# Graph convolution with residual and layer norm: comparison columns in a PSUM bank, and picks in six turns of two and two sets

## The chip, the core and the metric

The kernel runs on one core of a Trainium2 chip. The core has a matrix engine (TensorE, PE in the profile; its weight loads are PEld), VectorE (DVE), ScalarE (ACT), GpSimd (POOL) and SyncE (SP), which run side by side and wait for one another through semaphores. Matmul results land in PSUM, which this kernel divides into eight banks of 512 fp32 columns on 128 partitions; everything else lies in SBUF. The metric is the device time of one execution in microseconds. A run's program is fixed before it starts: each engine works through its own list of instructions in that list's order.

## The reference

There are 12,500 nodes with 128 features and 400,000 edges sorted by destination. Each edge takes its source's row, multiplies it by one of two weight matrices by its type, and is summed into its destination; then come the self term, a relu, the residual and a layer norm.

```
Xs = X[src]
m_data = Xs @ W_data.T + b_data
m_ctrl = Xs @ W_control.T + b_control
msg = jnp.where((edge_types == 0)[:, None], m_data, m_ctrl)
agg = jax.ops.segment_sum(msg, dst, num_segments=X.shape[0])
out = relu(agg + (X @ W_self.T + b_self))
x = layernorm(x + out)
```

## The kernel before

Sums over edges are linear, so the kernel first adds up source rows by destination and type, and multiplies by the weights afterwards. Rows of x are kept in SBUF as three bf16 parts whose sum is the fp32 value (`x3`: block of 128 nodes, part, feature).

The 3,125 chunks of 128 edges fall into 25 groups of 125. A part of each group's chunks has its source rows fetched by GpSimd's indirect DMAs (`msg`, line 887; 945 of them). The others, twenty chunks at a time, form 109 **pairs** (windows of 2,560 edges), whose source rows come out of SBUF by matmul. For a pair VectorE works out where each edge goes: it compares every edge's block number with a column of block numbers (`O`, 2,000 wide, `block_matrix`), gets ranks from a prefix sum that TensorE makes of `O` (`before`, line 634, in the bank `side`; VectorE reads it in `ahead`, line 642, and goes on with `product`, the folds of lines 656 and 661, `found`, `rank`, `rm`), and multiplies (`rv`, line 713). TensorE then **puts** the edges into slots (line 726), ScalarE copies the slots (`cell`), a DMA writes them out and another spreads them over the partitions, and VectorE turns them into one-hot columns (`pick`, line 790). This is prepared one to three pairs ahead.

With the pick columns TensorE **picks** (line 990): 25 sets of slots, each set four matmuls that write 32 partitions each and 384 columns (three parts of a row), of which the last set has two matmuls. ScalarE copies the picked rows from PSUM to bf16 (`emsg`, lines 1004 and 1006). VectorE makes a selection per set by comparing the codes of its slots with `code_col` (`esel`, 172 wide for one set, line 541 of the helper `select`), and TensorE **adds** (line 803): three matmuls a set, rows times selection, into a bank `sums`. At the end of a pair VectorE adds the bank to the accumulators (`acc`, line 876, 172 columns). Fetched chunks go the same way, with `psel` (compared with `near_col`) and matmuls 48 wide.

A pair's picks run in five turns of 5, 5, 5, 4 and 5 sets (`bounds`); the half set goes with the fourth turn. A turn picks two sets into a tile of two banks (`got2`), two or three into a tile of three banks (`got3`), and ScalarE makes one copy of each. In the same turn the sets of the turn before are added; a pair's last sets are added in the first turn of the next pair. Each of the two tiles has one buffer, so a turn's picks wait for the copy of the turn before. The eight banks are: `side` 1, `sums` 2, `got2` 2, `got3` 3. Selections are made in three instructions, for 10, 9 and 6 sets.

What sets the order: the code gives each piece of work a place within its pair (`merged`, fractions of a pair; for example the second selection 0.305, `ahead` 0.31, the third selection 0.36), some VectorE work is chained in a fixed order (`in_turn`), and a scheduler then decides each engine's list before the run, by priority and by its own estimate of when things are ready. Work may therefore stand far ahead of the place at which the code writes it.

## Time and profile before

| | us |
|---|---|
| median of 3 runs (1672.21 to 1674.59) | 1673.62 |
| the profiled execution | 1674.38 |
| its span (first to last instruction) | 1672.7 |
| of it 0 to 100: rows are split into parts, first pairs prepared | VectorE busy 84.8, TensorE 45.7 |
| of it 1600 to 1672.7: last pairs, last rows written | VectorE busy 43.1, TensorE 62.4 |
| mean granted TensorE clock | 0.994 |

Outside its span the profiled execution has 1.7 us. In the long middle one pair follows another every 14 us or so, and every engine's load is nearly even over it. In the rows below, the number behind an x is a count; behind a bar stand the busy time in us and the mean duration of one instruction in ns, and behind the next bar how long the engine stood idle before such instructions, and what ended the idling.

### The profile page before, as it was taken

How to read it: one execution, taken by the hardware profiler on the slowest of the kernel's cores; microseconds unless marked ns; L12 is line 12 of the kernel's file. 1: busy time of each engine (PE TensorE's matmuls, PEld its weight loads, DVE VectorE, ACT ScalarE, POOL GpSimd, SP SyncE). 2: the span in 40 equal slices, each digit the busy share in tenths (PEclk: the TensorE clock that was granted, in tenths of full speed). 3: DMA queues.
4: the chain of work that ended last, by engine and by line, in shares of the span. 5: the costliest groups of instructions: out<-in, count | busy, mean ns of one | idle time of the engine just before them, and what ended most of it. 6: DMA issues, size and time to landing. Idle time of an engine off the chain costs nothing.

```text
span 1672.7 us, 67703 instructions
## 1 busy us (share of the span) xinstructions
PE 1551.5 (93%) x27966; PEld 1222.6 (73%) x27966; DVE 1569.9 (94%) x4078; ACT 1224.0 (73%) x2056; POOL 1239.8 (74%) x1022
## 2 busy tenths in 40 slices
PE   1699999999999999999999999999999999999998
PEld 0377777777777777777777777777777777777776
DVE  9799999999999999999999999999999999999983
ACT  7687777777777777677777778767786777668674
POOL 1277777887887887778777887878887787877881
PEclk9899999999999999999999999999999999999999
DMA  7944444554455454544554454554545454544441
GB/s 218 278 148 139 130 150 132 153 154 135 142 160 151 137 158 132 155 135 133 159 149 140 137 155 138 151 160 132 159 125 163 137 160 129 160 138 136 137 134 42
DMA packets 147605, 246.05 MB, mean 147 GB/s; under 512 B 35565, under 2 KB 114264, under 8 KB 147288
## 3 DMA queue, kind: packets, MB, share of 16 engines
q1 hardware_dynamic: 99128, 142.50, 25.6%
q0 software_dynamic: 48160, 99.14, 22.4%
q8 instruction: 221, 3.62, 0.9%
q14 instruction: 96, 0.79, 0.1%
HBM read 224.04 MB, written 17.52 MB: 144 GB/s over the span
## 4 chain that ended last, share of the span: by engine, by line
DVE 42%; PE 41%; issue 6%; ACT 5%; DMA 3%; DVEq 1%; POOL 0%; SPq 0%; ACTq 0%; POOLq 0%
PE sums L803 18%; PE got L990 13%; DVE esel L541 6%; DVE prod L656 4%; PE side L1111 4%; DVE prod L648 4%; DVE pick L790 3%; DVE O L541 3%; ACT emsg L1004 2%; DVE rv L713 2%; DVE prod L627 2%; DVE psel L541 2%; DVE rm L541 2%; DVE found L666 2%; PE side L726 2%
## 5 line engine op out<-in xcount | busy, mean ns | idle before, releaser
L887 POOL DMA_INDIRECT msg<-rows,idx_g x945 | 1169.2, 1237 | 311.5 <-issue 122.8
L1004 ACT CAST emsg<-got 128x768 bf16<-128x768 f32 x1090 | 965.3, 930 | 295.4 <-PE got L990 286.4
L803 PE MATMUL sums<-esel,emsg 128*128 128x172 bf16 x7848 | 687.2, 238 | 5.4 <-DVE acc L876 4.3
L803 PEld LDWEIGHTS <-emsg 128*128 128x128 bf16 x7848 | 569.0, 97 | 118.0 <-issue 109.5
L990 PE MATMUL got<-x,pick 128*32 128x384 bf16 x10682 | 582.1, 330 | 11.6 <-ACT emsg L1004 6.2
L990 PEld LDWEIGHTS <-pick 128*32 128x32 bf16 x10682 | 246.4, 96 | 140.1 <-issue 20.1
L541 DVE TENSOR_TENSOR esel<-code_col,code 128x1720 bf16<-128x1720 bf16 x327 | 292.9, 896 | 5.6 <-PE sums L803 5.3
L803 PE MATMUL sums<-psel,msg 128*128 128x48 bf16 x2835 | 161.8, 184 | 11.1 <-DVE acc L876 11.0
L803 PEld LDWEIGHTS <-msg 128*128 128x128 bf16 x2835 | 133.8, 97 | 20.0 <-issue 17.0
L656 DVE TENSOR_TENSOR prod<-prod 128x1200 bf16<-128x1200 bf16 x218 | 136.2, 625 | 9.7 <-issue 4.5
L648 DVE TENSOR_TENSOR prod<-O,ahead 128x2000 bf16<-128x2000 bf16 x109 | 130.7, 1199 | 2.8
L541 DVE TENSOR_TENSOR O<-cell_col,blk 128x2000 bf16<-128x2000 bf16 x109 | 129.8, 1190 | 0.5 <-ACT blk L443 0.5
L790 DVE TENSOR_SCALAR pick<-pick,lane_f 128x3200 bf16<-128x3200 bf16 x109 | 112.7, 1034 | 2.6 <-DMA pick<-there 2.6
L726 PE MATMUL side<-rv,O 128*128 128x64 bf16 x2180 | 85.4, 196 | 31.4 <-DVE rv L713 30.9
L963 POOL DMA_INDIRECT both<-rows,idx x55 | 65.5, 1190 | 65.7 <-DVE mv L1125 27.5
L726 PEld LDWEIGHTS <-O 128*128 128x128 bf16 x2180 | 80.1, 100 | 38.9 <-DVE rv L713 27.7
L541 DVE TENSOR_TENSOR psel<-near_col,near 128x1200 bf16<-128x1200 bf16 x125 | 95.9, 767 | 0.0
L627 DVE TENSOR_TENSOR prod<-prod 128x500 bf16<-128x500 bf16 x327 | 94.3, 288 | 0.8
L713 DVE TENSOR_TENSOR rv<-rm,vals 128x1280 bf16<-128x1280 bf16 x109 | 89.3, 820 | 0.0
L622 DVE TENSOR_TENSOR prod<-O 128x1000 bf16<-128x1000 bf16 x109 | 73.9, 678 | 2.4 <-DVE bits L701 1.0
L876 DVE TENSOR_TENSOR acc<-acc,sums 128x172 f32 (+2 forms) x234 | 65.4, 280 | 2.7 <-PE sums L803 2.5
L642 DVE TENSOR_REDUCE ahead<-side 128x100 bf16<-128x200 f32 x109 | 39.1, 359 | 26.0 <-PE side L634 24.8
(197 smaller groups left out, 1528.1 us busy)
## 6 DMA issues: line engine op xcount, KB each, us to landing
pick<-there SPq DMA_DIRECT2D x108, 800.0 KB
msg<-rows,idx_g POOLq DMA_INDIRECT x945
acc<-acc_start SPq DMA_DIRECT2D x23, 640.0 KB
rows<-x SPq DMA_DIRECT2D x6, 1344.0 KB
xs<-in_x_dram SPq DMA_DIRECT2D x99, 62.5 KB
out_dram<-h SPq DMA_DIRECT2D x99, 62.5 KB
xt<-in_x_dram SPq DMA_DIRECT2D x6, 896.0 KB
cnt<-cnt_start SPq DMA_DIRECT2D x22, 160.0 KB
```

The source lines that it names most:

```text
L541: ins = nc.vector.tensor_tensor(sel.rearrange("p n (w t) -> p n w t", t=2), col[:rows].rearrange("p (o w t) -> p o w t", o=1, t=2).to_broa ...
L622: return nc.vector.tensor_add(h[:, :2 * CQ], s["O"][:, :2 * CQ], s["O"][:, 2 * CQ:])
L627: return nc.vector.tensor_add(h[:, to:to + n], h[:, a:a + n], h[:, b:b + n])
L648: return nc.vector.tensor_tensor(s["prod"][:, :, :NCELL], s["O"], s["ahead_b"].rearrange("p (o j) -> p o j", o=1).to_broadcast([P, EC, NCE ...
L656: return nc.vector.tensor_add(prod[:, :, :h], prod[:, :, :h], prod[:, :, h:2 * h])
L713: placed[:] = [nc.vector.tensor_tensor(rv.rearrange("p c v (r t) -> p c v r t", t=2), s["rm"].rearrange("p c (o r t) -> p c o r t", o=1, t ...
L726: nc.tensor.matmul(s["rk"][:m, :2 * CAP], s["held"][:, c * NCELL:c * NCELL + m], s["rv"][:, c].rearrange("p v r -> p (v r)"), start=(c == ...
L790: return nc.vector.tensor_scalar(t, t, lane_f, None, op0=OP.is_equal)
L803: last = nc.tensor.matmul(out, msg[:, j * D:(j + 1) * D], sel, start=(start and j == 0), stop=stop, skip_group_check=True)
L887: return nc.gpsimd.indirect_dma_start(out=msg, out_offset=None, in_=rows3[:, :], in_offset=bass.IndirectOffsetOnAxis(ap=codes["p", g][0][: ...
L990: last = nc.tensor.matmul(ps[CAP * a:CAP * (a + 1), :], slots[w]["pick"][:, a * NQ + q, :], x3[:, 4 * q + a - a0].rearrange("p j d -> p (j ...
L1004: s["out"] = nc.scalar.copy(msg[:, :n], ps[:, :n, :3 * D])
```

## The change

It does three things.

1. A new pool holds one PSUM bank, `cols`. The five tables that VectorE compares with (two of `cell_cols`, `rank_col`, `code_col`, `near_col`) are copied there once, as fp32 words, and `select` reads them from there as bf16. The compared codes still come from SBUF.
2. The picks run in six turns of four sets, each turn with two tiles of two banks (`got0`, `got1`). The half set is picked in the fifth turn as six matmuls of 128 columns, into the 128 columns that are left free in three of the four banks; ScalarE copies it with two instructions in place of one. The selections are made for 8, 8 and 9 sets. What was tied to the fourth and fifth turn (put, spread, codes) is tied to the fifth and sixth.
3. Each pick is ordered behind the pick before it and given high priority (`behind`), over a whole tile.

The banks are now `side` 1, `sums` 2, `got0` 2, `got1` 2, `cols` 1.

```diff
@@ -218,6 +218,7 @@
     ps1 = ctx.enter_context(tc.tile_pool(name="ps1", bufs=1, space=PSUM))
     ps2 = ctx.enter_context(tc.tile_pool(name="ps2", bufs=2, space=PSUM))
     psg = ctx.enter_context(tc.tile_pool(name="psg", bufs=1, space=PSUM))
+    psc = ctx.enter_context(tc.tile_pool(name="psc", bufs=1, space=PSUM))
 
     def side():
 
@@ -351,6 +352,18 @@
     rank_col = table(CAP, 0, "rank_col")
     code_col = table(2 * EW, 1, "code_col")
     near_col = table(2 * PW, 0, "near_col")
+    cols = psc.tile([P, 512], FP, name="cols")
+
+    def on_psum(t):
+        n = t.shape[1] // 2
+        at = cols[:, used[0]:used[0] + n]
+        used[0] += n
+        nc.vector.tensor_copy(at, t.bitcast(FP))
+        return at.bitcast(BF)
+
+    used = [0]
+    cell_cols = [on_psum(t) for t in cell_cols]
+    rank_col, code_col, near_col = on_psum(rank_col), on_psum(code_col), on_psum(near_col)
     ident_b = keep.tile([P, P], BF, name="ident_b")
     nc.vector.tensor_copy(ident_b, ident)
     lane_f = keep.tile([P, 1], FP, name="lane_f")
@@ -765,9 +778,9 @@
             keep_codes()
             s["own"][3]()
 
-        s["tiled"] = {4: [put, spread], 5: [turn_codes, keep_codes]}
+        s["tiled"] = {5: [put, spread], 6: [turn_codes, keep_codes]}
         if w % 2:
-            s["tiled"][5] = [lambda: (turn_codes(), own_before())]
+            s["tiled"][6] = [lambda: (turn_codes(), own_before())]
             s["own_turn"] = own_turn
         wide = NCELL + EC
         s["begin"] = {"blocks": block_matrix, "same": same_lane, "tens": tens, **{
@@ -971,12 +984,12 @@
 
         g, i = each_e[w]
         s = {"sel": {}, "msg": {}}
-        bounds = [0, 5, 10, 15, 19, NQ - 1]
+        bounds = [0, 4, 8, 12, 16, 20, NQ - 1]
         turns = len(bounds) - 1
 
         def choose(q0, n, prev=None):
 
-            sel = sp.tile([P, 10, 2 * EW], BF, name="esel", bufs=3)[:, :n]
+            sel = sp.tile([P, 9, 2 * EW], BF, name="esel", bufs=3)[:, :n]
             sel, ins = select(sel, code_col, slots[w]["code"][:, q0:q0 + n], prev)
             for k in range(n):
                 s["sel"][q0 + k] = sel[:, k]
@@ -985,25 +998,38 @@
         lead = 0 if w % 2 else 2
         half_rows = slice(CAP * lead, CAP * lead + OVF)
 
-        def pick(ps, q, a0=0, a1=4):
+        def behind(first, f):
+
+            if first is None:
+                return f()
+            with after(first), tc.high_priority():
+                return f()
+
+        def pick(ps, q, a0=0, a1=4, last=None):
             for a in range(a0, a1):
-                last = nc.tensor.matmul(
+                last = behind(last, lambda: nc.tensor.matmul(
                     ps[CAP * a:CAP * (a + 1), :], slots[w]["pick"][:, a * NQ + q, :],
                     x3[:, 4 * q + a - a0].rearrange("p j d -> p (j d)"), start=True, stop=True, skip_group_check=True,
-                )
+                ))
             return last
 
-        def rows(q, n, room, half=False):
-            ps = psg.tile([P, room, 512], FP, name=f"got{room}")
-            msg = two.tile([P, room, 3 * D], BF, name=f"emsg{room}")
-            for k in range(n):
-                last = pick(ps[:, k, :3 * D], q + k)
-                s["msg"][q + k] = msg[:, k, :]
+        def rows(q, k, half=False):
+            ps = psg.tile([P, 2, 512], FP, name=f"got{k}")
+            msg = two.tile([P, 2, 3 * D], BF, name=f"emsg{k}")
+            last, ends = None, (2 - k) if half else 0
+            for j in range(ends):
+                for a in range(lead, lead + 2):
+                    last = behind(last, lambda: nc.tensor.matmul(
+                        ps[CAP * a:CAP * (a + 1), j, 3 * D:], slots[w]["pick"][:, a * NQ + NQ - 1, :],
+                        x3[:, 4 * (NQ - 1) + a - lead, 2 * k + j, :], start=True, stop=True, skip_group_check=True,
+                    ))
+            for j in range(2):
+                last = pick(ps[:, j, :3 * D], q + j, last=last)
+                s["msg"][q + j] = msg[:, j, :]
+            s["out"] = nc.scalar.copy(msg, ps[:, :, :3 * D])
             if half:
-                last = pick(ps[:, n, :3 * D], NQ - 1, lead, lead + 2)
-            s["out"] = nc.scalar.copy(msg[:, :n], ps[:, :n, :3 * D])
-            if half:
-                nc.scalar.copy(s["msg"][NQ - 1][half_rows, :], ps[half_rows, n, :3 * D])
+                to = s["msg"][NQ - 1][half_rows, 2 * k * D:(2 * k + ends) * D]
+                nc.scalar.copy(to.rearrange("p (k d) -> p k d", d=D), ps[half_rows, :ends, 3 * D:])
             return last
 
         def add(q0, q1):
@@ -1015,17 +1041,17 @@
 
         def unit(t):
 
-            if t == 3:
+            if t == 4:
                 assert not spare
                 if "both" in slots[w]:
                     slots[w]["last"] = two.tile([P, 3 * D], BF, name="last", bufs=1)
                 s["msg"][NQ - 1] = slots[w]["last"]
-            paced(w + (t + 0.5) / turns, rows(bounds[t], 2, 2))
+            paced(w + (t + 0.5) / turns, rows(bounds[t], 0, t == 4))
             if t == 1 and w > 0 and w % 2 == 0:
                 spare.append(lambda: spare_rows(w))
-            gate = rows(bounds[t] + 2, bounds[t + 1] - bounds[t] - 2, 3, t == 3)
+            gate = rows(bounds[t] + 2, 1, t == 4)
             if t == 0:
-                choose(0, 10)
+                choose(0, 8)
                 gates = ending() or [gate]
             while counts:
                 c = counts.pop(0)
@@ -1037,8 +1063,6 @@
             if t > 0:
                 gates = add(bounds[t - 1], bounds[t])
             paced(w + (t + 1) / turns, gates[0])
-            if t == 2:
-                paced(w + (t + 1) / turns, gates[-1])
             for u in tiled.get(t, []):
                 u()
             if t == 0 and w + 1 < pairs and "own_turn" in slots[w + 1] and w > 0:
@@ -1057,7 +1081,7 @@
             accumulate(place_of(g, 2 * i + 1), acc_rows(g, 0, 2), s["ps"], EW, EW)
             return gates
 
-        chosen_later = [lambda prev=None, q=q, n=n: choose(q, n, prev) for q, n in ((10, 9), (19, NQ - 19))]
+        chosen_later = [lambda prev=None, q=q, n=n: choose(q, n, prev) for q, n in ((8, 8), (16, NQ - 16))]
         return evenly([lambda t=t: unit(t) for t in range(turns)]), end, chosen_later
 
 
@@ -1154,7 +1178,7 @@
             at["rk"] = side()
             s[2]()
 
-        return {5: [lambda: None, turn, s[3]]}, [(0.1, before), (0.33, s[1])]
+        return {6: [lambda: None, turn, s[3]]}, [(0.1, before), (0.33, s[1])]
 
     def check_all():
```

What this does to the lists of instructions, at three places in the middle of the program:

VectorE, around the read of the prefix sum (`ahead`), before. TENSOR_LOAD and ISA read a window's place into a register; `prod` 20x60, 20x30 and 20x14 are the folds.

```order
L642 TENSOR_REDUCE ahead<-side 128x100
L648 TENSOR_TENSOR prod<-O,ahead 128x20x100
L859 TENSOR_LOAD place_i
L859 ISA x2
L656 TENSOR_TENSOR prod<-prod 128x20x60
L541 TENSOR_TENSOR esel<-code_col,code 128x1032
L656 TENSOR_TENSOR prod<-prod 128x20x30
L541 TENSOR_TENSOR esel<-code_col,code 128x1720
L661 TENSOR_TENSOR prod<-prod 128x20x14
L666 TENSOR_REDUCE found<-prod 128x20
L612 TENSOR_TENSOR prod<-blk_21792,blk_184 128x20x20
L671 CAST rank<-found 128x40
```

The same place now.

```order
L554 TENSOR_TENSOR esel<-cols,code 128x1376
L655 TENSOR_REDUCE ahead<-side 128x100
L661 TENSOR_TENSOR prod<-O,ahead 128x20x100
L872 TENSOR_LOAD place_i
L872 ISA x2
L669 TENSOR_TENSOR prod<-prod 128x20x60
L554 TENSOR_TENSOR esel<-cols,code 128x1548
L669 TENSOR_TENSOR prod<-prod 128x20x30
L674 TENSOR_TENSOR prod<-prod 128x20x14
L679 TENSOR_REDUCE found<-prod 128x20
L625 TENSOR_TENSOR prod<-blk_22380,blk_193 128x20x20
L684 CAST rank<-found 128x40
```

Before, the third selection of a pair (1032) and the first of the next (1720) stand between the folds; now only the third (1548) does, and the last two folds follow each other directly.

VectorE, at the end of a pair: the accumulations (`acc`, `cnt`), before. `prod` 2x100 and 100 are the last two folds of the next prefix sum's input.

```order
L627 TENSOR_TENSOR prod<-prod 128x2x100
L541 TENSOR_TENSOR esel<-code_col,code 128x1548
L627 TENSOR_TENSOR prod<-prod 128x100
L876 ISA
L876 TENSOR_TENSOR acc<-acc,sums 128x2x86
L876 ISA
L876 TENSOR_TENSOR cnt<-cnt,sums 64x120
L876 ISA
L876 TENSOR_TENSOR acc<-acc,sums 128x2x40
L541 TENSOR_TENSOR psel<-near_col,near_21340 128x1200
```

The same place now; the row `esel` 1376 that leads the listing above follows directly behind it.

```order
L554 TENSOR_TENSOR esel<-cols,code 128x1376
L640 TENSOR_TENSOR prod<-prod 128x2x100
L581 TENSOR_SCALAR om_all_202<-slot_col,side 128x70
L640 TENSOR_TENSOR prod<-prod 128x100
L581 TENSOR_SCALAR om_all_202<-slot_col,side 128x70
L889 ISA
L889 TENSOR_TENSOR acc<-acc,sums 128x2x86
L554 TENSOR_TENSOR psel<-cols,near_20270 128x1200
L889 ISA
L889 TENSOR_TENSOR cnt<-cnt,sums 64x120
L889 ISA
L889 TENSOR_TENSOR acc<-acc,sums 128x2x40
```

Ahead of `ahead` there was one selection (1548, the pair's second); now there are two, the pair's first and second (1376 each). The first has moved here from behind the previous pair's third.

TensorE, where it makes the prefix sum (`ltri` is its weight), before.

```order
L990 LDWEIGHTS pick
L990 MATMUL got_19830<-x_104,pick 32x384
L634 LDWEIGHTS ltri
L634 MATMUL side<-prod,ltri 128x2x25
L634 LDWEIGHTS ltri
```

And now, at such a place.

```order
L816 LDWEIGHTS emsg_20272
L816 MATMUL sums<-esel,emsg_20272 128x172
L647 LDWEIGHTS ltri
L647 MATMUL side<-prod,ltri 128x2x25
L647 LDWEIGHTS ltri
```

Before, it stands right behind a turn's picks in 67 of the 109 pairs, and behind adds in 8; now behind picks in 38, and behind adds in 51.

## The prediction

> **What bounds the kernel now.** I read the page's busy shares first, then the busy time of the long middle, then who waits for whom there, because shares over the whole span mix the start and the tail with it.
>
> ```profile
> PE 1551.5 (93%) x27966; PEld 1222.6 (73%) x27966; DVE 1569.9 (94%) x4078; ACT 1224.0 (73%) x2056; POOL 1239.8 (74%) x1022
> DVE 42%; PE 41%; issue 6%; ACT 5%; DMA 3%; DVEq 1%; POOL 0%; SPq 0%; ACTq 0%; POOLq 0%
> 100.00:1600.00 1500.00, 1443.41 (x26322) 1141.15 (x26312) 1442.01 (x3691) 1111.18 (x1894) 1180.70 (x955) 1.00 0.48 144
> DVE ahead L642 <- PE side L634: 22.3, 33, 1.9
> DVE esel L541 <- PE sums L803: 0.9, 2, 0.8
> PE side L574 <- DVE om_all L568: 15.4, 18, 1.0
> PE sums L803 <- DVE acc L876: 15.0, 29, 1.9
> PE got L990 <- ACT emsg L1004: 4.3, 7, 1.3
> ```
>
> The second row is the chain that ended last, by engine; the third is the stretch from 100 to 1600 us (busy PE, PEld, DVE, ACT, POOL); the others are waits in that stretch (us, times, longest). TensorE and VectorE are both busy for 96% of it, and the chain passes between them. VectorE is the tighter one, since TensorE's busy time covers waits inside its pipelined matmuls. VectorE stands idle for 1500 − 1442.0 = 58.0 us, and the largest item is `ahead` waiting for TensorE's prefix sum, 22.3 us. ScalarE and GpSimd have 389 and 319 us to spare. So the time is VectorE's work plus what VectorE waits for, and a change must shorten one of the two.
>
> **Part 1: the columns in PSUM.** 670 instructions change their first source: `O`, `rm` and three `esel` 109 times each, `psel` 125 times.
>
> ```profile
> L541 DVE TENSOR_TENSOR O<-cell_col,blk 128x2000 bf16<-128x2000 bf16 x109 | 129.8, 1190 | 0.5 <-ACT blk L443 0.5
> L541 DVE TENSOR_TENSOR esel<-code_col,code 128x1720 bf16<-128x1720 bf16 x109 | 114.0, 1046 | 5.5 <-PE sums L803 5.3
> L541 DVE TENSOR_TENSOR esel<-code_col,code 128x1548 bf16<-128x1548 bf16 x109 | 103.9, 953 | 0.1
> L541 DVE TENSOR_TENSOR esel<-code_col,code 128x1032 bf16<-128x1032 bf16 x109 | 75.0, 688 | 0.0
> L876 DVE TENSOR_TENSOR acc<-acc,sums 128x172 f32 x109 | 35.3, 324 | 2.7 <-PE sums L803 2.5
> L876 DVE TENSOR_TENSOR acc<-acc,sums 128x240 f32 x16 | 6.2, 390 | 0.0
> L839 DVE TENSOR_TENSOR acc<-acc 128x280 f32<-128x280 f32 x24 | 10.5, 436 | 0.0
> ```
>
> From 1032 to 2000 columns a selection grows by 502 ns, 0.519 ns a column, with a fixed 152 ns. No row reads bf16 from PSUM. The nearest are `acc`, one fp32 source in PSUM (`sums`) and one in SBUF: 0.97 ns a column and, at 1.04, 145 ns fixed for 172 columns; L839, both sources in SBUF, has 436 − 280 × 1.04 = 145 as well. So the place of a source moves the fixed part by nothing that shows, and I take 0. The bounds: the fixed part could fall to 145, 670 × 7 ns = 5 us less; or the rate could fall to the fp32 rows' one column per 1.04 ns, twice as slow.
>
> [...]
>
> [...]
>
> The five copies that fill `cols` cost some 0.1 us each, once, 0.5 us. Whatever GpSimd gains from a freer VectorE cannot count: it is idle for a fifth of the middle, and no fetched chunk is among the waits above.
>
> **Part 2: VectorE's list.** The selections still cover 25 × 172 columns in three instructions, so their work is unchanged. Two things in their place are not.
>
> ```profile
> 815.67 0.77 DVE L541 TENSOR_TENSOR psel<-near_col,near 128x1200 bf16<-128x1200 bf16 x1
> 816.36 0.35 DVE L642 TENSOR_REDUCE ahead<-side 128x100 bf16<-128x200 f32 x1
> 816.75 1.20 DVE L648 TENSOR_TENSOR prod<-O,ahead 128x2000 bf16<-128x2000 bf16 x1
> 817.99 0.79 DVE L656 TENSOR_TENSOR prod<-prod 128x1200 bf16<-128x1200 bf16 x1
> ```
>
> An instruction normally starts 0.08 us before the end of the one in front (815.67 + 0.77 against 816.36); one that needs its neighbour's result starts 0.04 us after it (816.75 + 1.20 against 817.99). A dependent neighbour therefore costs 0.12 us. Over the whole list such neighbours go from 489 to 556, mostly because the first selection no longer stands between the last fold and `found`: 67 × 0.12 = **+8.0 us** of VectorE time, on the tighter engine, with nothing to hide it.
>
> Against this, the moved selection changes when VectorE asks for the prefix sum. Between `ahead` and `rv` stood 1720 and 1032, now 1548; ahead of `ahead` stood 1548, now 1376 twice. With 0.08 us of overlap each, 0.966 + 0.608 − 0.873 = 0.70 us per pair moves from behind `ahead` to in front of it. VectorE reaches `ahead` 0.70 us later in its own list, without more work in all.
>
> **Part 3: TensorE's list.**
>
> ```profile
> 803.30 0.39 PE L803 MATMUL sums<-psel,msg 128*128 128x48 bf16 x9
> 803.61 1.00 PE L990 MATMUL got<-x,pick 128*32 128x384 bf16 x20
> 804.54 1.29 PE L803 MATMUL sums<-esel,emsg 128*128 128x172 bf16 x15
> 805.67 0.24 PE L803 MATMUL sums<-psel,msg 128*128 128x48 bf16 x3
> 805.83 1.00 PE L990 MATMUL got<-x,pick 128*32 128x384 bf16 x18
> ...
> 63.97 0.51 PE L990 MATMUL got<-x,pick 128*32 128x384 bf16 x8
> 64.41 0.54 PE L803 MATMUL sums<-esel,emsg 128*128 128x172 bf16 x5
> ```
>
> Starts count here, since the ends are modelled. Five sets take 804.54 − 803.61 = 0.93 us until the next kind of work, two sets 0.44: 0.163 a set and 0.11 for the change of work behind them. Nine `psel` matmuls take 0.31 until picks follow, three take 0.16: 0.025 each, and 0.085 for the change into picks. A batch of picks thus costs 0.20 us beyond its sets. In the two lists batches go from 630 to 727: +97 × 0.20 = 19.4 us. But 78 batches used to break inside a set of four, which then streams twice, and now none does: −78 × 0.163 = −12.7 us. The half set's six narrow matmuls stream the columns of the two wide ones; 0. Together +6.7 us on TensorE, half a percent of its work, and it lies beside VectorE's work, under 56.6 us of TensorE idling (1500 − 1443.4). If that cover were gone it would cost 6.7 us.
>
> For the prefix sum TensorE is earlier: in the two turns in front of it there are eight picks (0.33 us) and three adds fewer (three of 15 in 1.13 us, 0.22); six adds (0.45 us) now precede it in 51 of 109 pairs, 0.21 on average. Net 0.34 us earlier. With VectorE's 0.70 us, the margin at `ahead` grows by some 1.0 us against waits of 22.3 / 33 = 0.68 us on average and 1.9 at most. Nearly all the short ones go, the long ones keep up to 0.9; some of the waits will turn up later, at `acc` or at a gap that VectorE reaches sooner. I take **−15 us** of the 22.3, bounds 0 and −22.3.
>
> **Part 4: ScalarE.**
>
> ```profile
> L1004 ACT CAST emsg<-got 128x768 bf16<-128x768 f32 x654 | 512.3, 801 | 270.5 <-PE got L990 262.5 <-PE sums L803 1.3 <-ACT emsg L1004 1.0
> L1004 ACT CAST emsg<-got 128x1152 bf16<-128x1152 f32 x436 | 489.5, 1123 | 24.9 <-PE got L990 23.9 <-PE side L747 0.2 <-issue 0.2
> L1006 ACT CAST both<-got 64x384 bf16<-64x384 f32 x55 | 26.5, 481 | 0.0
> ```
>
> Per pair six copies of 801 and four of 1123 (9298 ns) become twelve of 801 (9612). The half set's copy of about 480 becomes two, 256 and 128 columns wide; at (1123 − 801) / 384 = 0.84 ns a column and 157 fixed they take 372 + 264. That is +0.47 us a pair, 52 us in all, inside the 389 us that ScalarE idles. What it can cost is the second rival's case.
>
> **Sum.** 1674.38 (profiled, 0.76 above the median) − 15 + 8.0 + 0.5 + 0 = 1667.9, I say **1668 us**, 0.4% down.
>
> **Rivals.**
>
> *The waits only move* (25%). The first selection used to be made one stretch ahead (in the list, behind the third); now it stands just in front of `acc`, with two to three us until its adds. If VectorE is late there, TensorE waits for it, and `ahead` or `acc` waits in turn for TensorE. That `esel` and `sums` hardly waited for each other before (0.9 us) speaks for room; that TensorE already waits 15.0 us for `acc` speaks against. Then the −15 is void: 1674.4 + 8.5 = 1683 us.
>
> *Slower: four banks hand over too tightly* (12%). Behind the last pick of one `got1`, TensorE needs 0.11 + 12 adds (0.90) + a few `psel` matmuls with the change (0.16 to 0.24) + two sets (0.33) = 1.50 to 1.58 us until the next `got1`. ScalarE's two copies take at most 2 × 0.80 us and start 0.33 earlier, and I allow 0.2 for noticing: ready at 1.47. The margin is 0.03 to 0.11 us. Before it was 1.73 to 1.81 (three adds more, 0.23) against 0.80 + 1.12 − 0.49 + 0.2 = 1.63, so 0.10 to 0.18, and cost 4.3 us of waits. ScalarE's other work is (1224.0 − 965) / 109 = 2.4 us a pair, and it decides as soon as a piece over 0.2 us falls into a turn without other TensorE work. Lost in half of the 654 turns, 0.2 us makes 65 us; 40 of them fit into TensorE's idling. 1674.4 + 8.5 + 25 = 1708 us.
>
> *The PSUM source runs at the slow rate* (6%). 906,000 selected columns × 0.519 ns = 470 us, all on VectorE: about 2140 us. For it: no bf16 row from PSUM shows the fast rate. Against: nothing in the `acc` rows shows a PSUM port slower than SBUF's at the same type.
>
> *The PSUM source is a little cheaper and the waits go* (9%): 1668 − 5 − 7 = 1656 us.
>
> **Chances and range.** The forecast, 1660 to 1676, has 46%; two percent are left for what I did not think of. Faster by over 0.2% (below 1671, about what a measurement can tell from no change) holds the last rival and most of the forecast: 48%. Within 0.2%: the forecast's upper part and a mild form of the first rival, 17%. Slower: 35%. The range of 1650 to 1694 leaves out the slow rate, most of the tight hand-over and a few percent below; its low end is all 22.3 us gone with the cheaper source, its high end the first rival plus TensorE's uncovered 6.7 us and a few.
>
> **What would show it.** In the changed kernel's profile, part 1 is right if `O<-cols` takes 1180 to 1195 ns. Part 2: VectorE's busy time stays within 5 us of 1569.9, `ahead` waits under 8 us, and neighbours such as `found` behind the fold of L674 start 0.04 us after it. Part 3: 20 matmul picks become 16 in about 0.76 us. The second rival shows as picks that wait for `emsg` by tens of us, the first as `sums` waiting for `esel` or more for `acc`. I am wrong if VectorE's idling in the middle does not fall.

## The result, and the profile after

| | before | after |
|---|---|---|
| median, us | 1674.11 (4 runs, 1672.21 to 1676.89) | 1700.14 (4 runs, 1698.8 to 1700.63) |
| ratio | | 1.0151, interval 1.0135 to 1.0166 |
| span of the profiled execution, us | 1672.7 | 1698.0 |
| mean granted TensorE clock | 0.994 | 0.996 |

The change makes the kernel 1.5% slower, 26 us, outside the predicted range. In two of the sessions reported further down every kernel, the one before included (1947 us), took 16 to 19% longer, with instructions about as long and more idling between them (one kernel's VectorE was busy for 1565 us of a span of 1942 there, e13b, and for 1549 of 1675 otherwise, e13c); ratios from there are given, and not set beside the others. Of the changed kernel, the page's busy shares and chain, then the stretch from 100 to 1600 us (busy PE, PEld, DVE, ACT, POOL), and from that stretch the waits that answer to those shown of before:

```profile
PE 1579.8 (93%) x28402; PEld 1222.2 (72%) x28402; DVE 1577.6 (93%) x4083; ACT 1259.7 (74%) x2383; POOL 1069.9 (63%) x1022
PE 53%; DVE 25%; ACT 10%; issue 7%; DMA 2%; POOL 1%; DVEq 1%; SPq 0%; ACTq 0%; POOLq 0%
100.00:1600.00 1500.00, 1446.47 (x26258) 1122.18 (x26259) 1426.30 (x3642) 1125.01 (x2166) 999.95 (x940) 1.00 0.48 142
DVE ahead L655 <- PE side L647: 22.5, 38, 1.5
PE got L1010 <- ACT last L1032: 22.3, 46, 0.6
PE got L1010 <- ACT emsg L1029: 10.5, 27, 0.9
PE got L1010 <- ACT both L1032: 3.8, 19, 0.3
PE side L587 <- DVE om_all L581: 3.9, 11, 0.8
PE sums L816 <- DVE acc L889: 0.8, 2, 0.6
```

The chain has turned over: TensorE 53 and ScalarE 10%, VectorE 25, where it was 41, 5 and 42. Picks now wait for ScalarE's copies by 36.6 us (22.3 + 10.5 + 3.8) against 4.3. `last` and `both` at L1032 are the half set's narrow copies. TensorE's waits for VectorE have gone the other way, `om_all` from 15.4 to 3.9 and `acc` from 15.0 to 0.8 us: that was the idling meant to cover TensorE's extra work, and most of it is used up. `ahead` waits as long as it did. VectorE's idling in this stretch, which the prediction made the sign of its being wrong, rises from 58.0 to 73.7 us (1500 − 1426.3).

Three groups of the changed kernel by shape (count, then busy us and mean ns of one, then idle time before them):

```profile
L554 DVE TENSOR_TENSOR O<-cols,blk 128x2000 bf16<-128x2000 bf16 x109 | 129.7, 1190 | 0.5 <-ACT blk L456 0.5
L1032 ACT CAST last<-got 64x256 bf16<-64x256 f32 x54 | 19.9, 368 | 1.3
L1032 ACT CAST last<-got 64x128 bf16<-64x128 f32 x54 | 14.1, 261 | 1.3
```

`O` takes 1190 ns from PSUM as it did from SBUF. The two narrow copies take 0.63 us (368 + 261 ns), as estimated (372 + 264).

To see what that does, one turn of the changed kernel on the timeline, ScalarE first (start, duration, engine, line, operation):

```profile
817.63 0.80 ACT L1029 CAST emsg<-got 128x768 bf16<-128x768 f32 x1 [0.49 <-PE got L1010]
818.46 0.37 ACT L1032 CAST last<-got 64x256 bf16<-64x256 f32 x1
818.85 0.80 ACT L1029 CAST emsg<-got 128x768 bf16<-128x768 f32 x1
819.67 0.26 ACT L1032 CAST last<-got 64x128 bf16<-64x128 f32 x1
```

```profile
817.42 0.49 PE L1010 MATMUL got<-x,pick 128*32 128x384 bf16 x6
817.85 1.07 PE L816 MATMUL sums<-esel,emsg 128*128 128x172 bf16 x12
818.78 0.31 PE L816 MATMUL sums<-psel,msg 128*128 128x48 bf16 x6
819.01 0.51 PE L1010 MATMUL got<-x,pick 128*32 128x384 bf16 x8
819.98 0.51 PE L1010 MATMUL got<-x,pick 128*32 128x384 bf16 x8 [0.46 <-ACT last L1032]
```

The fifth turn's picks are over when the adds begin, at 817.85; the next turn's come at 819.01 and fill `got0`, which is free. For `got1` they stand until 819.98, because four copies run one behind another and the last of them, 0.26 us for a third of half a set, still reads that tile. Without the narrow copies it would have been free at about 819.3, an estimate: 818.46 and a wide copy's 0.80 us.

Neighbouring sets of one batch of picks normally start 0.15 to 0.16 us apart, for which 0.158 is taken (from a set's last pick to the next set's first the median is 0.153 in the traces of before and after, from first pick to first 0.163). Every gap over 0.17 us between the starts of neighbouring picks of a batch, less these 0.158, added up over a trace, gives the picks' waits as one number (behind a batch's eighth pick is where `got1` begins). It is used below: 17.6 us in 98 gaps before, 59.9 in 152 after, 44.2 of it behind the eighth pick of batches of sixteen.

### The profile page after: what moved, and what is told of

Same layout as the page of the kernel before. It is cut to its first block, busy times and chain, and to the rows that moved or that the text cites. A ratio compares the mean times of both kernels' runs of the same rounds, so it can differ in the third digit from the quotient of the medians.

```text
span 1698.0 us, 69059 instructions
## 1 busy us (share of the span) xinstructions
PE 1579.8 (93%) x28402; PEld 1222.2 (72%) x28402; DVE 1577.6 (93%) x4083; ACT 1259.7 (74%) x2383; POOL 1069.9 (63%) x1022
## 3 DMA queue, kind: packets, MB, share of 16 engines
q0 software_dynamic: 48160, 99.14, 22.1%
## 4 chain that ended last, share of the span: by engine, by line
PE 53%; DVE 25%; ACT 10%; issue 7%; DMA 2%; POOL 1%; DVEq 1%; SPq 0%; ACTq 0%; POOLq 0%
PE sums L816 23%; PE got L1010 17%; ACT emsg L1029 6%; PE side L1135 4%; DVE esel L554 3%; PE side L739 2%; DVE prod L669 2%; DVE prod L661 2%; DVE pick L803 2%; DMA msg<-rows,idx_g 2%; PE sums L931 2%; DVE O L554 1%; DVE rv L726 1%; ACT last L1032 1%; PE side L587 1%
## 5 line engine op out<-in xcount | busy, mean ns | idle before, releaser
L900 POOL DMA_INDIRECT msg<-rows,idx_g x945 | 992.3, 1050 | 467.2 <-PE got L1010 176.8
L1029 ACT CAST emsg<-got 128x768 bf16<-128x768 f32 x1308 | 998.4, 801 | 308.6 <-PE got L1010 283.7
L816 PE MATMUL sums<-esel,emsg 128*128 128x172 bf16 x7848 | 716.2, 238 | 1.3 <-DVE acc L889 0.8
L1010 PE MATMUL got<-x,pick 128*32 128x384 bf16 x10464 | 599.4, 330 | 45.0 <-ACT last L1032 25.0
L554 DVE TENSOR_TENSOR esel<-cols,code 128x1376 bf16<-128x1376 bf16 x327 | 292.0, 893 | 0.6 <-issue 0.6
L816 PE MATMUL sums<-psel,msg 128*128 128x48 bf16 x2835 | 175.8, 184 | 0.2
L816 PEld LDWEIGHTS <-msg 128*128 128x128 bf16 x2835 | 142.8, 97 | 17.3 <-issue 14.3
L554 DVE TENSOR_TENSOR O<-cols,blk 128x2000 bf16<-128x2000 bf16 x109 | 129.7, 1190 | 0.5 <-ACT blk L456 0.5
L554 DVE TENSOR_TENSOR psel<-cols,near 128x1200 bf16<-128x1200 bf16 x125 | 96.2, 770 | 1.1 <-issue 1.1
L635 DVE TENSOR_TENSOR prod<-O 128x1000 bf16<-128x1000 bf16 x109 | 73.7, 676 | 1.8 <-DVE bits L714 0.3
L747 ACT CAST cell<-side 128x64 bf16<-128x64 f32 x109 | 23.5, 216 | 65.8 <-PE side L739 63.0
```

Source lines behind the costliest of these rows:

```text
L554: ins = nc.vector.tensor_tensor(sel.rearrange("p n (w t) -> p n w t", t=2), col[:rows].rearrange("p (o w t) -> p o w t", o=1, t=2).to_broa ...
L635: return nc.vector.tensor_add(h[:, :2 * CQ], s["O"][:, :2 * CQ], s["O"][:, 2 * CQ:])
L816: last = nc.tensor.matmul(out, msg[:, j * D:(j + 1) * D], sel, start=(start and j == 0), stop=stop, skip_group_check=True)
L900: return nc.gpsimd.indirect_dma_start(out=msg, out_offset=None, in_=rows3[:, :], in_offset=bass.IndirectOffsetOnAxis(ap=codes["p", g][0][: ...
L1010: last = behind(last, lambda: nc.tensor.matmul(ps[CAP * a:CAP * (a + 1), :], slots[w]["pick"][:, a * NQ + q, :], x3[:, 4 * q + a - a0].rea ...
L1029: s["out"] = nc.scalar.copy(msg, ps[:, :, :3 * D])
```

## The experiments

All ratios are to the kernel before, run on the same chip in the same session; e1 to e15 are names of runs. Unless it is said otherwise, before took 1673.4 to 1674.8 us there.

**One part undone or alone.** Tables from SBUF, the eighth bank unused (e1):

```diff
-    cell_cols = [on_psum(t) for t in cell_cols]
-    rank_col, code_col, near_col = on_psum(rank_col), on_psum(code_col), on_psum(near_col)
```

> The changed kernel with the five comparison tables read from SBUF again; six turns, four pick banks and the tied picks stay, the eighth bank is empty. Hand-off theory (TensorE waits inside its batches of picks for ScalarE's copies, 60 us against 18 before): nothing of that is touched, so 1695 to 1703 us, and waits inside batches of 50 to 65 us. List theory (the PSUM columns cost through the order that the scheduler gives VectorE, 67 more dependent neighbours): dependent neighbours fall back to the count of before, 8 us or more come back, 1685 to 1692 us. O<-cell_col at 1190 ns in both: the memory of the source has no price of its own. GpSimd's fetches go back from 1050 to about 1240 ns, without effect on the time.

1696.23 us, 1.0121 (1.0099 to 1.0144); picks' waits 54.7 us. The columns are not where the 26 us are. A fetch takes 1261 ns again.

On top of that, the half set as two wide matmuls into the freed bank, with one copy of 64x384 (e2):

```diff
+                own = psh.tile([P, 512], FP, name="got_half")
+                last = pick(own[:, :3 * D], NQ - 1, lead, lead + 2, last=last)
...
+                nc.scalar.copy(s["msg"][NQ - 1][half_rows, :], own[half_rows, :3 * D])
```

> As e1, but the bank that is left over takes the half set: two wide matmuls and one ScalarE copy of 384 columns in place of six narrow matmuls and two narrow copies that hold got0 and got1. Hand-off theory: the 30 us in which picks wait for the narrow copies go, so 20 to 30 us below e1: 1670 to 1680 us. Batch theory (the loss is the fixed cost of six batches a pair in place of five, some 19 us of TensorE): the batches stay at 690 to 700, so within 5 us of e1.

1682.57 us, 1.0038 (1.0023 to 1.0054); picks' waits 11.4 us. That is a little above the 1670 to 1680 expected. Still six turns of four sets, but one copy that holds neither tile and stands behind both wide copies: 14 of e1's 22 us are gone. Of the picks' waits 43 us are gone; waits elsewhere take the place of a part, on TensorE for `acc` (1.2 to 7.3 us) and for `om_all` (12.7 to 17.1).

The changed kernel without the tie (e3):

```diff
-            with after(first), tc.high_priority():
-                return f()
+            return f()
```

> The changed kernel without the tie between picks (no order, no priority); all else stays. Its list has 773 batches of picks instead of 727, with sets broken up again. Batch theory: +46 x 0.20 us and about 90 broken sets x 0.163 us = +24 us of TensorE, which is the tighter engine now: 1715 to 1725 us. Hand-off theory: batches that are broken up give ScalarE more time, so part of the 60 us of waits goes: 1695 to 1710 us.

1717.05 us, 1.0244 (1.022 to 1.0269). The tie is worth 17 us here; without it there are 773 batches of picks in TensorE's list instead of 727, and 111 of them end inside a set that a later batch takes up again.

The tie alone, in the kernel before (`behind` around its matmuls in `pick`; e4):

> The kernel before with the tie between picks alone (five turns, five pick banks, tables in SBUF). Its list has 577 batches in place of 630 and no set broken up: 53 x 0.20 + 78 x 0.163 = 23 us less TensorE work. If VectorE sets the pace, as the prediction had it: 1668 to 1676 us, no change. If TensorE's work counts as much: 1650 to 1660 us.

1670.96 us, 0.9973 (0.9958 to 0.9988), with 577 batches instead of 630. A small gain, and the fastest kernel of this study.

**The half set's copies, none and twice.** First without them (e5):

```diff
-                nc.scalar.copy(to.rearrange("p (k d) -> p k d", d=D), ps[half_rows, :ends, 3 * D:])
...
-                s["msg"][NQ - 1] = slots[w]["last"]
+                s["msg"][NQ - 1] = no_rows
```

> The changed kernel without ScalarE's two narrow copies of the half set (a tile of zeros is added up in their place, so the half set's rows are missing from the sums); its six matmuls stay. Theory 'hand-over': the second tile's buffer comes free 0.59 us earlier in the fifth turn (326 + 262 ns), so of the 59.9 us that picks wait inside their batches at most 12 stay, and the time falls by some 15 us, to 1680 to 1688 us. Theory 'six turns alone' (more batches and list order cost the time, ScalarE's copies lie beside other work): within 4 us of 1700, and the picks' waits stay above 40 us.

1673.72 us, 0.9997 (0.9985 to 1.001): the whole loss is gone, more than the 12 to 20 us expected. Its chain and three of its waits in the stretch from 100 to 1600 us:

```profile
PE 42%; DVE 41%; issue 6%; ACT 6%; DMA 2%; DVEq 1%; POOL 1%; SPq 0%; ACTq 0%; POOLq 0%
PE got L1012 <- ACT emsg L1031: 10.9, 32, 0.6
PE side L589 <- DVE om_all L583: 11.6, 19, 1.1
PE sums L818 <- DVE acc L891: 6.1, 12, 0.8
```

The chain is split as before, and TensorE has part of its waits for VectorE back (15.4 and 15.0 us before). Then each narrow copy twice (e6):

```diff
+                for _ in range(2):
+                    nc.scalar.copy(to.rearrange(...), ps[half_rows, :ends, 3 * D:])
```

> The changed kernel with each of the two narrow copies issued twice. ScalarE gets 65 us more work and has over 300 to spare. Theory 'hand-over': the second tile is released another 0.59 us later in each of 109 pairs, nothing of it is slack any more, so 64 us more of picks' waits, of which other waits on TensorE give back a third or so: 1730 to 1765 us, with 110 to 130 us of waits inside batches. Theory 'six turns alone': within 4 us of 1700.

1721.07 us, 1.0281 (1.0259 to 1.0302). The chain of this kernel:

```profile
PE 60%; ACT 16%; DVE 15%; issue 6%; DMA 2%; DVEq 1%; POOL 0%; SPq 0%; ACTq 0%; POOLq 0%
```

None, one and two of each make 1674, 1700 and 1721 us: close to a line. The second pair cost 21 us, less than expected. It stands wholly behind both wide copies, in every pair: ScalarE's order is wide, 256, wide, 256, 128, 128. So `got1`'s wide copy is as early as in the changed kernel, and what grows is the time for which both tiles are held. The picks' waits have moved with it: 30.7 us inside batches, and some 54 beyond the usual gap in front of a batch's first pick (9 in the changed kernel), since `got0` now comes free late too.

**Time on ScalarE, or a tile held?** The narrow copies read a constant in SBUF, so that nothing ties them to the two tiles (e10, repeated as e10b and e10c):

```diff
-                nc.scalar.copy(to.rearrange("p (k d) -> p k d", d=D), ps[half_rows, :ends, 3 * D:])
+                nc.scalar.copy(to, x3[half_rows, k].rearrange("p j d -> p (j d)")[:, :ends * D])
```

> The changed kernel with the two narrow copies at their places and of their sizes, but reading a constant in SBUF (so the half set's rows in the sums are wrong); they keep ScalarE busy and no longer hold got0 and got1. Theory 'ScalarE's order': the second tile's wide copy still stands behind the first narrow copy, but the second narrow copy no longer delays its release, so 0.33 of the 0.59 us stay: 1684 to 1692 us and 20 to 40 us of waits inside batches. Theory 'banks held': what counts is that a tile is not released before its narrow copy has been made, and ScalarE's time is covered: 1674 to 1680 us, as without the copies. Theory 'ScalarE's time': any 0.59 us there costs the same: 1696 to 1702 us.

In the first of the two sessions in which the kernel before took 1947 us: 2011.53 us, 1.0322. In the second:

> The kernel of e10 again, likewise: the narrow copies read a constant in SBUF (the half set's rows in the sums are wrong), so they keep ScalarE busy and do not hold got0 and got1. 'ScalarE's order' (0.33 of the 0.59 us stay): 1684 to 1692 us, 20 to 40 us of waits inside batches. 'Banks held': 1674 to 1680. 'ScalarE's time': 1696 to 1702.

2006.79 us, 1.0306. And where before took 1673.48:

> The kernel of e10 once more, since its first two chips were ones on which the kernel before took 1947 us (the narrow copies read a constant in SBUF; the half set's rows in the sums are wrong). If before takes about 1674 us here: 'ScalarE's order' 1684 to 1692 us and 20 to 40 us of waits inside batches; 'banks held' 1674 to 1680; 'ScalarE's time' 1696 to 1702. The ratios of 1.031 of the two runs before speak for the third.

1684.48 us, 1.0066 (1.0042 to 1.0089), picks' waits 25.6 us. The time is the one that the theory of ScalarE's order gave, but the run does not test that theory, because the scheduler moved the copies. Free of the tiles, they no longer stand in the fifth turn. An excerpt of ScalarE's timeline, with other instructions between its rows left out:

```profile
814.42 0.40 ACT L1032 COPY both<-x 64x256 bf16<-64x256 bf16 x1
814.74 1.48 ACT L1029 CAST emsg<-got 128x768 bf16<-128x768 f32 x2
816.21 0.30 ACT L1032 COPY both<-x 64x128 bf16<-64x128 bf16 x1
```

Here they stand in front of a turn's two wide copies and behind them; over the whole run they stand between two pairs or behind one of a pair's first three turns. In the changed kernel the copy 256 wide stands between the fifth turn's two wide copies in all 109 pairs; here a narrow copy stands between two wide copies of a turn once in 218 times. The two also take 0.70 us together in place of 0.63. So the run shows that as much of ScalarE's time in other turns, holding no tile, costs 11 us (against e5), and that their place in the fifth turn together with their hold on the tiles costs the other 16. Of these two the doubled copies speak for the hold; how the 16 us divide stays open.

**Six turns and the columns, without those copies.** The kernel of e5 with the tables in SBUF (e14, repeated as e14b and e14c):

> The changed kernel without the narrow copies (the half set's rows are missing from the sums) and with the tables read from SBUF: six tied turns of four banks and nothing else of the change. Theory 'six turns cost 10 us by themselves' (the step from the tied kernel before, 1671, to the one with the half set in a bank of its own, 1683): 1678 to 1684 us. Theory 'the half set's copy is all': 1668 to 1676, within 5 us of the same kernel with the columns in PSUM (1674). A difference between these two of more than 4 us is what the columns' place does.

> The kernel of e14 again, on a chip on which the kernel before takes about 1674 us: six tied turns, tables in SBUF, no narrow copies (the half set's rows are missing from the sums). 'Six turns cost 10 us by themselves': 1678 to 1684 us. 'The half set's copy is all': 1668 to 1676. More than 4 us from the same kernel with the columns in PSUM (1674) is what the columns' place does.

> The kernel of e14 once more, likewise (six tied turns, tables in SBUF, no narrow copies; the half set's rows are missing from the sums). If before takes about 1674 us here: 'six turns cost 10 us by themselves' 1678 to 1684 us; 'the half set's copy is all' 1668 to 1676. Its ratios of 1.013 and 1.015 so far speak for the first, though they were measured where every kernel is slower.

In the two sessions with 1947 us before: 1974.88 and 1975.67 us (1.0151 and 1.0131). With 1673.48 before: 1690.66 us, 1.0107 (1.0073 to 1.0142). It was expected at 1684 at most, and it is 17 us slower than the same kernel with the columns in PSUM. The picks' waits are only 10.2 us, but ScalarE stands still elsewhere. Its copy of fetched rows (`last<-both`, every other pair) in this kernel, then in the changed one:

```profile
L1067 ACT COPY last<-both 64x384 bf16<-64x384 bf16 x54 | 27.6, 511 | 20.9 <-DMA both<-rows,idx 20.9
```

```profile
L1072 ACT COPY last<-both 64x384 bf16<-64x384 bf16 x54 | 27.6, 512 | 0.0
```

The longest of those stalls on the timeline of e14c, on GpSimd, ScalarE and TensorE:

```profile
893.81 1.59 POOL L898 DMA_INDIRECT msg<-rows,idx_g  x1 [0.30 <-PE got L1008]
895.71 0.94 POOL L898 DMA_INDIRECT msg<-rows,idx_g  x1 [0.30 <-issue]
896.95 0.94 POOL L974 DMA_INDIRECT both<-rows,idx  x1 [0.30 <-issue]
898.20 0.94 POOL L898 DMA_INDIRECT msg<-rows,idx_g  x1 [0.30 <-issue]
```

```profile
895.75 0.21 ACT L745 CAST cell<-side 128x64 bf16<-128x64 f32 x1 [0.58 <-PE side L737]
902.22 0.51 ACT L1067 COPY last<-both 64x384 bf16<-64x384 bf16 x1 [6.26 <-DMA both<-rows,idx]
902.63 1.48 ACT L1027 CAST emsg<-got 128x768 bf16<-128x768 f32 x2
```

```profile
903.47 1.52 PE L1008 MATMUL got<-x,pick 128*32 128x384 bf16 x16 [5.06 <-ACT emsg L1027]
```

GpSimd starts the fetch at 896.95, with others right in front of it and behind it; the rows land at 902.2. ScalarE, which takes its list in order, waits 6.26 us for them, and behind it wait two copies of picks, and the picks, 5.06 us. The fetch itself is a short one, 0.94 us; one in front of it took 1.59 us. With the tables in PSUM the fetches are shorter on average (1048 ns in e5, 1257 in e14c), and this copy never waits in any of the kernels measured with 1674 us before (the changed one, e3, e5, e6, e10c), while with the tables in SBUF it waits 7.5 to 20.9 us in all that have it. To see what the wait costs, the copy was left out (e15):

```diff
-            if t == turns - 1 and "both" in slots[w]:
-                with after(slots[w + 2]["kept"] if w + 2 < pairs else s["out"]):
-                    nc.scalar.copy(slots[w]["last"][:OVF, :], slots[w]["both"][:OVF, :])
```

> The kernel of e14c (six tied turns, tables in SBUF, no narrow copies) also without ScalarE's copy of the fetched rows of every other pair into 'last' (54 copies of 0.51 us, whose result that kernel doesn't use; the half set's rows are missing from the sums). In e14c ScalarE stood 20.9 us in front of this copy, 8 times and up to 6.3 us, waiting for GpSimd's fetch, and picks waited up to 5.1 us behind it; with the columns in PSUM, where a fetch takes 1050 instead of 1257 ns, it never waits. Theory 'late fetch': the 17 us between this kernel's two forms are that wait, so without the copy 1672 to 1679 us (up to 5 of it for the copies' own time), and the waits at 'ahead' fall from 39.7 to under 30. Theory 'the list' (the 17 us come from another order of VectorE's and TensorE's work): 1685 to 1691.

1677.72 us, 1.0023 (1.001 to 1.0036); `ahead` waits 25.0 us instead of 39.7. The late fetch is up to 13 of the 17 us (the 54 copies' own time, 27.6 us of ScalarE, is in this too). In e2 the same copy waits 16.5 us, so part of what still separates e2 from e5 may be that.

**VectorE's list.** The selections for 8, 8 and 9 sets in the tied kernel before (e7), and in the kernel before itself (e9):

```diff
-                choose(0, 10)
+                choose(0, 8)
...
-        chosen_later = [lambda prev=None, q=q, n=n: choose(q, n, prev) for q, n in ((10, 9), (19, NQ - 19))]
+        chosen_later = [lambda prev=None, q=q, n=n: choose(q, n, prev) for q, n in ((8, 8), (16, NQ - 16))]
```

> The kernel before with its picks tied and the selections made for 8, 8 and 9 sets: five turns, five banks, columns in SBUF. If the selections' sizes matter by dependent neighbours on VectorE, as the prediction priced them, its list now says 438 against 457 of the tied kernel and 473 of before: 19 x 0.12 = 2 us less than 1671, so 1667 to 1671 us. If the moved selection takes away waits for the prefix sum, as the prediction had it, the 30.9 us of waits at 'ahead' fall below 15 and the time to 1655 to 1662.

> The kernel before with selections for 8, 8 and 9 sets and nothing else. By the prediction's part 2: waits at 'ahead' fall from 22.3 to under 8 us and the time to 1659 to 1665 us. By its first rival (waits only move): 1672 to 1680 us, 'ahead' waits as before or others in their place. Dependent neighbours in VectorE's list are 446 against 473, worth 3 us of gain by the 0.12 us each.

1675.89 us, 1.0013 (0.9998 to 1.0028), and 1677.07, 1.0019 (1.0006 to 1.0031). The wait for the prefix sum, of e7 and of e9:

```profile
DVE ahead L642 <- PE side L634: 33.3, 38, 2.0
```

```profile
DVE ahead L642 <- PE side L634: 24.5, 37, 1.6
```

The sizes alone take nothing off the wait, in either kernel, and cost 5 and 3 us. But they do not move the first selection either. In their lists it stands in front of `ahead` in 5 and 4 of 109 pairs (before: 2); in the changed kernel it does so in 108, and with the tables back in SBUF (e1) in 2. So the move that the prediction priced comes with the columns' place, and these two runs don't test it. The kernels that do differ in it, e4 for comparison, then e1 without the move, e15 without and e5 with it:

```profile
DVE ahead L642 <- PE side L634: 30.9, 38, 2.7
DVE ahead L651 <- PE side L643: 31.1, 42, 1.5
DVE ahead L653 <- PE side L645: 25.0, 30, 1.5
DVE ahead L657 <- PE side L649: 17.1, 29, 1.4
```

From e1 to the changed kernel (22.5) and from e15 to e5 the wait falls by some 8 us, in kernels that differ in the columns' place too (e15 also lacks a copy). The tie alone had raised it by as much, from 22.3 to 30.9.

Last, less work for VectorE in the tied kernel: the final step of the layer norm as scale and bias on ScalarE (e13, repeated as e13b and e13c).

```diff
-                nc.vector.tensor_scalar(
-                    h[:r, i, :], h[:r, i, :], mv[:r, i, 0:1], rs[:r, i:i + 1], op0=OP.subtract, op1=OP.mult
-                )
+                nc.scalar.activation(h[:r, i, :], h[:r, i, :], AF.Identity, bias=low[:r, i:i + 1], scale=rs[:r, i:i + 1])
...
+            nc.vector.scalar_tensor_tensor(low[:rows, :k], mv[:rows, :k, 0], -1.0, rs[:rows, :k], op0=OP.mult, op1=OP.mult)
```

> The kernel before, tied, with the last step of the layer norm (subtract the mean, times the deviation's inverse) made by ScalarE as scale and bias in place of VectorE: about 24 us less for VectorE, about 30 us more for ScalarE in 101 pieces. If VectorE sets the pace of the tied kernel (58% of its chain): 1650 to 1660 us. If the pieces on ScalarE come between picks and their copies and cost as much there: 1668 to 1675.

> The kernel of e13 again, likewise: the kernel before, tied, with the last step of the layer norm on ScalarE, 24 us less for VectorE and 30 us more for ScalarE. If VectorE sets the pace of the tied kernel: 1650 to 1660 us. If the pieces on ScalarE cost as much between picks and copies: 1668 to 1675.

> The kernel of e13 once more (the kernel before, tied, with the last step of the layer norm on ScalarE: some 25 us less for VectorE, 41 us more for ScalarE at the 485 ns that one took). On the two chips where before took 1947 us it was level with before. If before takes about 1674 us here and VectorE sets the pace of the tied kernel: 1650 to 1662 us. If the pieces on ScalarE come between picks and their copies and cost as much there as VectorE gains: 1668 to 1676.

In the two sessions with 1947 us before: 1945.56 and 1944.45 us, level with it (1.000 and 0.9985). With 1674.78 before: 1672.98, 0.9988 (0.9977 to 1.0), 2 us above the tied kernel without it, though VectorE's busy time fell from 1566.8 to 1548.8. In the window from 100 to 1600 us:

```profile
DVE ahead L642 <- PE side L634: 38.7, 41, 2.7
PE got L997 <- ACT emsg L1012: 8.8, 21, 1.3
```

In the tied kernel these two are 30.9 and 3.6 us. What VectorE saved came back as waiting. ScalarE got 38 us more work at the same time, and picks wait 5 us more for its copies; how much of the saving that ate, and how much TensorE's pace, this run does not separate.

## Why the prediction was wrong

The steps from before to after, by the medians:

| step | runs | us, about |
|---|---|---|
| picks tied | before to e4 | −4 |
| six turns, four banks, new selections | e4 to e14c | +20, of it up to 13 the late fetch (e15) |
| columns in PSUM | e14c to e5 | −17 |
| the half set's narrow copies | e5 to the change | +26 |

The steps are not independent. With the narrow copies in place the columns' move made no gain at all (e1 to the change, +4 us, the intervals overlapping), and with the tables in SBUF taking the narrow copies out saved only 6 us (e1 to e14c), while ScalarE's waits for the late fetch rose from 9.2 to 20.9 us. So 26 us is what the copies cost in the kernel as it was changed. Of the second step some 5 us may be the new selections, which cost that much in five turns (e4 to e7).

**Part 4 is the step that failed**: it put the half set's two copies at nothing, and the price of the second rival that should have held them was taken from ordinary turns. The prediction called ScalarE's 52 us hidden "inside the 389 us that ScalarE idles", and weighed its pieces as a pair's average in ordinary turns, where the margin is 0.03 to 0.11 us. But it had placed both copies itself: they stand in the fifth turn, one between the two wide copies and one behind them, in every pair. With its own figures that turn's second tile is ready at 1.47 + 0.372 + 0.264 = 2.11 us, against 1.50 to 1.58 at which TensorE wants it: late by 0.53 to 0.61 us, in all of 109 pairs, 58 to 66 us. The 0.2 us for noticing in the 1.47 was the author's estimate; in the changed kernel's trace a copy that had waited for picks starts 0.11 us behind the end of the pick before it, and a pick that had waited for a copy 0.05 us behind the copy's end (medians). Less the 40 that it allowed for TensorE's idling, that is 18 to 26 us: 1674.4 + 8.5 + 18 to 26 = 1701 to 1709. The change came to 1700. So the rival was right in mechanism and nearly in price (1708), and "half of 654 turns" should have been "the one turn with the half set, always". The rows for that stood in the prediction; 12% was far too little. That the corrected sum lands so near is partly luck: picks waited 42 us more inside their batches, not 58 to 66, and TensorE's own work, which the sum leaves out, grew by 19 us (below). What the runs show in place of the step: without the two copies the loss is gone (1673.7 us), with each of them twice it is 47 us (1721.1), and in the changed kernel 26 us of the picks' waits (22.3 + 3.8) end with one of them.

**Part 1** held: 1190 ns for `O`, predicted 1180 to 1195. The third rival's slow rate (1.04 ns a column, put without its rows; `acc` before makes 1.06 from 80 to 240 fp32 columns, 220 to 390 ns) did not show: from `rm` to `O` (640 to 2000 columns, 490 to 1190 ns) a column takes 0.515 ns with one source in PSUM, and took 0.516 before. The five copies into `cols`, put at 0.1 us each with no row for it, took 0.17 to 0.25, 1.0 us together against the 0.5 in the sum. But "whatever GpSimd gains from a freer VectorE cannot count" was wrong in general. It counts where a fetch is late: ScalarE's waits for fetched rows were 8.3 us before and are none in the kernels with the columns in PSUM, and e14c against e5, with e15, puts up to 13 us on them in six turns.

**Part 2**, the 8.0 us: VectorE's busy time went from 1569.9 to 1577.6, just beyond the 5 us that the prediction gave as its own test, and the count held. Neighbours that start 0.025 to 0.07 us behind the end of the one in front number 487 in the trace of before and 545 in that of the changed kernel, and the largest rise is that of `found` behind the last fold (29 to 86), as the prediction said. Busy time holds only the 0.08 us of lost overlap, so the 58 more make 58 × 0.08 = 4.6 of its 7.7 us. What the prediction did not see is where they come from: the new sizes alone have 459 (e9), and with the tables back in SBUF there are 488 (e1). It is the columns' place that made the scheduler lay out another list; why it does so stays open.

**Part 3**, the −15 us at `ahead`, did not come: 22.3 before, 22.5 after. By the rows above, some 8 us go where the first selection moves, about half of the 15, and the tie had brought 8.6. The prediction worked out TensorE's lead at `ahead` from its list at that place alone, with its pace elsewhere as before. What else bounds the loop between the two was not tried further, and stays open.

TensorE's +6.7 us was mis-sized. Take, over the traces of before and after, the lower quartile of the gaps between the starts of each two kinds of neighbours as their usual gap, a set of picks counting as one, and call the usual gap work and what is beyond it waiting. Then TensorE's work grew by 18.7 us (22.1 by the median). The 97 batches at 0.20 make 19.4; the 12.7 to be won from broken sets, which rested on the author's estimate that such a set streams twice, did not show. In e4, with the 78 broken sets gone and 53 batches fewer, TensorE's work fell by 15.0 us (12.6 by the median), and the batches alone make 10.6 of it, which leaves 4.4 us (2.0) for the 78: a broken set costs little. And in the second rival the cover was counted twice, for this work and for the hand-over. TensorE's waits in all, by the same count, rose only from 162.4 to 168.5 us: with the 42 more inside batches, some 36 are gone elsewhere. Nothing hid the rest.

## What to carry over

Price a copy at the place where it stands: in a ring of buffers what counts is when the last reader of a tile is done in the one turn that has an extra reader, and an engine's idle time over the whole span says nothing about that turn (ScalarE had 389 us to spare, and copies of 0.63 us a pair cost 26 us). After every edit look where the scheduler has put the piece; an experiment that frees a copy from its tile also frees it to move. Free corners of a bank were not free storage here: what was put there held the tile until it was read, and picks waited 22.3 + 3.8 us for that. Where two engines feed each other, a saving on one of them can come back as waiting for the other, so test it alone before counting it (e13c, both 92% busy: 18 us less of VectorE's work than in e4, and no gain).

## What the hardware showed beside that

A bf16 comparison with one source in PSUM takes VectorE as long as with both in SBUF: 1190 ns for 2000 columns both ways, 770 against 767 for `psel`, 490 against 488 for `rm`. But GpSimd's indirect fetch, which shares no data with it, gets shorter; the group in the changed kernel and in e1, where only the tables' place differs:

```profile
L900 POOL DMA_INDIRECT msg<-rows,idx_g x945 | 992.3, 1050 | 467.2 <-PE got L1010 176.8 <-PE sums L816 154.9 <-issue 115.0
```

```profile
L896 POOL DMA_INDIRECT msg<-rows,idx_g x945 | 1191.3, 1261 | 305.7 <-issue 119.2 <-PE got L1006 71.1 <-PE sums L812 65.1
```

1050 against 1261 ns on average, 199 us of GpSimd's time; half of the fetches take 949 ns or less in the changed kernel, 1122 before. The difference goes with what VectorE does beside a fetch. Sorted by VectorE's instruction 0.1 us after the fetch began: in e1 the 60 fetches beside an idle VectorE take 955 ns on average, and the 312 beside one of the comparisons with a table take 1495; in the changed kernel the 406 beside such a comparison take 949. Beside `rv`, which has both sources in SBUF in either kernel, they stay long (21 fetches of 1531 ns on average in e1, 34 of 1617 in the changed kernel). So one source of 670 instructions left SBUF, and the fetches got 17% shorter; beside a comparison with a table in PSUM they are as short as the 37 beside an idle VectorE (948). Which part of the fetch waited was not measured.
